# The second mixture's outputs sent from slots to tokens by scatter, with the last two batches planned anew

## The chip, the cores and the metric

The kernel runs on one core of a Trainium2 chip. The metric is the device time of one launch in microseconds; the median of three runs is given. All numbers below come from those runs and from one further execution, recorded by the hardware profiler.

The core has TensorE (PE; its weight loads are listed apart as PEld), VectorE (DVE), ScalarE (ACT), GpSimd (POOL) and SyncE (SP). SP issues nearly all plain transfers and GpSimd all indirect ones. Sixteen DMA engines carry both.

## The reference

The input x has 8 sequences of 512 tokens, 128 wide, that is 4096 tokens. With LN for a layer norm without weights:

```
xn = LN(x)
s  = mamba(xn)        # projection, causal conv, a scan of 16 states for each of 256 channels, projection, norm, MLP
g  = silu(ffn0(xn))   # first mixture: 24 experts, top 2, two expert layers, 4 groups of tokens
x1 = x + s * g
xn = LN(x1)
s1 = attention(xn)    # causal, 8 heads of 128, after an RMS norm
y  = ffn1(xn)         # second mixture: 128 experts, top 2, one layer
out = x1 + s1 * silu(y)
```

The second mixture is what the change is about. Each expert has 32 places ("slots") for tokens that have it as first choice and 32 for those that have it as second; second choices count behind all first choices. A token beyond its expert's capacity is dropped:

```
v1, v2 = loc1 < 32, loc2 < 32
idx1, idx2 = e1 * 32 + min(loc1, 31), e2 * 32 + min(loc2, 31)
buf[idx1] += x * v1 ; buf[idx2] += x * v2
yb = buf (per expert, 32 x 128) @ we[expert]
y  = g1 * v1 * yb[idx1] + g2 * v2 * yb[idx2]
```

g1 and g2 are the two softmax weights, divided by their sum. loc2 starts at the number of all first choices of the expert, so a second choice's place is known only when all 4096 tokens are routed.

## The kernel before, in words

A batch is one sequence: 512 tokens, as four tiles of 128 rows (NJ = 4). Everything is float32 unless said otherwise.

**First part.** The first mixture runs expert by expert (`expert1` L435, `between` L453, `expert2` L504). Rows come by gathers of GpSimd (L128); each expert adds its bias by a small bf16 matmul with one-hot columns (L516 in `expert2`) ahead of the four products of L518. ScalarE's copy of an expert's transposed input is L444. `routing` also fills the table `xs_dram` with zeros (L405). Beside it the model part of the scan goes forward in steps (`front` L549, `scan` L589, `gated` L645, `back` L661). There are 64 steps, eight per batch. A step loads two states of B and C from memory (`bb`, `cb`), computes `da` on ScalarE (L601) and on VectorE a product (L603), scans (L605) and a second product (L606), and adds up on TensorE (`py`, L627). `front` approximates a logarithm by four squares on ScalarE (L581), each with an operation of VectorE (L582). `squares` in the change is the list of these.

**Middle part.** For each batch `fetch` (L522) and `after` (L537) bring together the first mixture's output (`o`, rows gathered by GpSimd at L131) and the scan's output (`sb`, `xb`) into x1. `Attention.prepare` (L747) norms x1, computes the 128 router logits, picks two experts per token and ends in `route` (L788). `route` counts places by prefix sums and sends each token's normed row to its two slots: eight scatters of GpSimd per batch (L828) into `xs_dram[0]` (first choices) and `xs_dram[1]` (second choices), with a spare row for dropped tokens. A table `row1` (from `pos` and `e12`) keeps where each token's two results will stand.

`Attention.heads` (L894) yields once per head. Per head: scores `sc` (L854), a mask with running minimum on VectorE (L856), exponentials on ScalarE (L860), transposes `pp` (L874) copied out as `pT` (L876), products `po` (L881), a reciprocal (L886) and `s` (L892). `values_of` (L832; `pv` L839, `v` L840) and the `qm` products (L846) belong to it too. After a batch's last head `s1` is stored.

The first six batches' heads (48) are emitted in turn with the scan steps that are left, in proportion: step by step the scan is kept level with heads out of 48. Batch b + 1 is fetched, gated and prepared at heads 1, 3 and 4 of batch b. The order of instructions on each engine follows this order of emission roughly; a scheduler moves an instruction ahead of others where it takes that one to be ready sooner.

```
    left = NSTEP - taken
    total = EARLY * HEADS
    for i in range(total):
        next(attention_steps)
        while (taken - (NSTEP - left)) * total < (i + 1) * left:
            step()
```

**Last part.** Then batch 7 is prepared, `weights2` (L912) turns router maxima into two weights per token for all batches, and `places` (L925) computes `live`: which second-choice slots lie behind the first choices. The list `second` is emitted one entry per head of batches 6 and 7: `slots` (L951) loads 512 slots of both tables and transposes them, `experts` (L968) multiplies eight experts' 64 slots each (`pye` L973), masks by `live` into `yb` (L975) and stores to `yb_dram` (L976). After the 16 groups of experts `finish` (L978) follows for batches 0 to 5, one per head, and for 6 and 7 at the very end. It gathers two rows per token (L128), multiplies by the weights (L990, L991), applies silu (L992), multiplies with `s1` (L993), adds x1 (L994) and stores the output (L995).

SP's queue holds all plain loads and stores in the order of emission, each behind the wait of the one ahead of it: `we` weights of the experts, `xg` of `slots`, `yb_dram` stores, the loads of `finish`, the output.

Of the kernel before, what the change touches and what calls it, by code (L numbers as in the profile page):

```python
# [33 lines left out]
S1 = E1 * C1  # L34
HEADS, DHEAD = 8, 128
# [12 lines left out]
def tile_kernel(ctx: ExitStack, tc: tile.TileContext, t: dict, out: bass.AP):  # L48
# [42 lines left out]

    xs_dram = [dram.tile([S1 + P, D], F32, name=f"xs_dram{k}") for k in range(2)]
    yb_dram = dram.tile([2 * S1, D], F32, name="yb_dram")

# [75 lines left out]
    w121 = w3.tile([P, NTT, 2], F32, name="w121")  # L170
    row1 = w3.tile([P, NTT, 2], I32, name="row1")
    idx1 = w3.tile([P, NTT, 2], I32, name="idx1")
    kp1 = w3.tile([P, NTT, 2], F32, name="kp1")
# [21 lines left out]
    bias = inv_pool.tile([3 * 32, DH + D], BF16, name="bias")  # L195
    zero = inv_pool.tile([P, L], F32, name="zero")
    G.memset(zero, 0.0)
# [106 lines left out]
    eb = xp.tile([3 * 32, DH + D], F32, name="eb", bufs=1)  # L304
    G.memset(eb, 0.0)
    for k in range(3):
        Q.dma_start(eb[32 * k : 32 * k + E0, 0:DH], t["eb1"])
        Q.dma_start(eb[32 * k : 32 * k + E0, DH:], t["eb2"])
    part = xp.tile([3 * 32, DH + D], BF16, name="part", bufs=1)
# [33 lines left out]
    def routing():  # L343
# [59 lines left out]
        for k in range(2):  # L403
            tc.keep_in_program_order(
                Q.dma_start(  # L405
                    xs_dram[k][0:S1, :].rearrange("(p n r) d -> p n (r d)", p=P, r=L // D),
                    bc(zero.unsqueeze(1), (P, S1 // L, L)),
                )
            )
# [25 lines left out]
    def expert1(e, w):  # L435

        we = w(e)
        px = ps_e.tile([P, SLOTS], F32, name="px", tag="pe")
        for c, r in enumerate(SROWS):
            xg = me.tile([CP, D], F32, name="xg", bufs=8)  # L440
            gather(xg[:r], xn_dram, inv[:r, c, e : e + 1])
            T.transpose(px[:, c * CP : c * CP + r], xg[:r], ident[:r, :r])  # L442
        xT = me.tile([P, SLOTS], F32, name="xTe", tag="xTe")
        S.copy(xT, px)  # L444
        hs = me.tile([CP, SG, DH], F32, name="hs", tag="big", bufs=4)
        for c, r in enumerate(SROWS):
            ph = ps_e.tile([CP, DH], F32, name="ph", tag="pe")
            T.matmul(ph[:r], chosen(e, r), bias[:, 0:DH], start=True, stop=False)
            T.matmul(ph[:r], xT[:, c * CP : c * CP + r], we, start=False, stop=True)  # L449
            S.activation(hs[:r, c, :], ph[:r], AF.Copy, scale=wsl[:r, c, e : e + 1])  # L450
        store(hs_dram, e, hs)
# [52 lines left out]
    def expert2(e, w):  # L504
# [4 lines left out]
        for c, r in enumerate(SROWS):  # L509
# [6 lines left out]
            T.matmul(po[:r, c, :], chosen(e, r), bias[:, DH:], start=True, stop=False)  # L516
            for f in range(NJ):
                T.matmul(po[:r, c, :], hT[:, f, :r], we[:, f, :], start=False, stop=(f == NJ - 1))  # L518
# [28 lines left out]


    def front(b):  # L549
# [30 lines left out]
        for i in range(4):  # L580
            S.activation(sq, ex, AF.Square, bias=l1p[:, i : i + 1], scale=LOG1P_S)  # L581
            V.scalar_tensor_tensor(lp, sq, LOG1P[i][1], ex if i == 0 else lp, ALU.add, ALU.mult)  # L582
# [157 lines left out]
    class Attention:  # L740
# [6 lines left out]
        def prepare(self, b, xb):  # L747

            at, (ps_x, px) = self.at, self.ps_x
            xn2 = at.tile([P, NJ, D], F32, name="xn2", bufs=1)  # L750
            layernorm(st, xb, xn2, NJ, eps5, "ln1")
            pt = ps_x.tile([P, L], F32, name="pt2", tag=px)
            for j in range(NJ):
                T.transpose(pt[:, j * P : (j + 1) * P], xn2[:, j, :], ident)
# [15 lines left out]

            sq = at.tile([P, NJ, D], F32, name="sq2", bufs=1)
            ss = st.tile([P, NJ], F32, name="ss2")
            for j in range(NJ):
                S.activation(sq[:, j, :], xn2[:, j, :], AF.Square, accum_out=ss[:, j : j + 1])
# [4 lines left out]
            V.tensor_tensor(sq, xn2, bc(ss.unsqueeze(2), (P, NJ, D)), ALU.mult)  # L779
# [8 lines left out]
        def route(self, b, xn2):  # L788
# [28 lines left out]
            kp = kp1[:, bs, :]  # L817
# [5 lines left out]
            for k in range(2):  # L823
                V.tensor_scalar(pos[:, :, k], pos[:, :, k], float(C1 - 1), float(k * C1), ALU.min, ALU.add)
            V.scalar_tensor_tensor(row1[:, bs, :], e12, float(2 * C1), pos, ALU.mult, ALU.add)  # L825
# [87 lines left out]
    def weights2():  # L913
        V.reciprocal(se1, se1)
        V.tensor_tensor(w121, mx1[:, :, 0:2], bc(mx1[:, :, 0:1], (P, NTT, 2)), ALU.subtract)
        S.activation(w121, w121, AF.Exp)
        V.tensor_tensor(w121, w121, bc(se1.unsqueeze(2), (P, NTT, 2)), ALU.mult)
        den = r3.tile([P, NTT], F32, name="den1")
        V.tensor_tensor(den, w121[:, :, 0], w121[:, :, 1], ALU.add)
        V.tensor_scalar(den, den, EPS32, None, ALU.max)  # L920
        V.reciprocal(den, den)
        V.tensor_tensor(w121, w121, bc(den.unsqueeze(2), (P, NTT, 2)), ALU.mult)
        V.tensor_tensor(w121, w121, kp1, ALU.mult)

    def places():  # L925


        pair = r3.tile([P, 2], F32, name="pair")
# [19 lines left out]
        V.tensor_scalar(live, pk, c, float(C1), ALU.add, ALU.is_lt)  # L948


    def slots(t):  # L951
        for k in range(2):
            xg = mo.tile([P, 4, D], F32, name="xg1", bufs=4)
            Q.dma_start(xg, rows(xs_dram[k][t * L : (t + 1) * L, :]))
            px = ps_x.tile([P, 4, P], F32, name="pxs", tag="px")
            for j in range(4):
                T.transpose(px[:, j, :], xg[:, j, :], ident)
# [11 lines left out]
    def experts(e0, we):  # L969
# [6 lines left out]
        Q.dma_start(rows(yb_dram[2 * C1 * e0 : 2 * C1 * (e0 + 8), :]), yb)  # L976

    def finish(b):  # L978
# [4 lines left out]
        y = mo.tile([P, NJ, D], F32, name="y", tag="y")  # L983
        for j in range(NJ):
            i = b * NJ + j
            ya = mo.tile([P, D], F32, name="ya", tag="row", bufs=6)
            yc = mo.tile([P, D], F32, name="yc", tag="row", bufs=6)
            gather(ya, yb_dram, row1[:, i, 0:1])
            gather(yc, yb_dram, row1[:, i, 1:2])
            V.tensor_scalar(ya, ya, w121[:, i, 0:1], None, ALU.mult)  # L990
            V.scalar_tensor_tensor(y[:, j, :], yc, w121[:, i, 1:2], ya, ALU.mult, ALU.add)  # L991
# [70 lines left out]
    for n, of in mixture():  # L1062
        due += n / of
        while due > 0.5:
            step()
            due -= 1.0
    moe.close()
# [21 lines left out]
    def early():  # L1089
        for b in range(EARLY):  # L1090
            for hd, _ in enumerate(beside.heads(b, ready[b])):
                if hd == 1:
                    got = fetch(b + 1)
                if hd == 3:
                    xb = after(b + 1, *got)
                if hd == 4:
                    ready[b + 1] = beside.prepare(b + 1, xb)
                yield

    left = NSTEP - taken  # L1100
    total = EARLY * HEADS
    attention_steps = early()
    for i in range(total):
        next(attention_steps)
        while (taken - (NSTEP - left)) * total < (i + 1) * left:
            step()
    for _ in model_steps:
# [16 lines left out]
    live = r3.tile([P, E1 // 2], F32, name="live")  # L1124
    loaded = {e0: load_experts(e0) for e0 in range(0, 32, 8)}
    last = Attention(at, m_qk, w_vo, (ps_x, "px"), (ps_q, "pq"), (ps_s, "ps"), (ps_t, "pt"), (ps_o, "po"))
    for b in range(EARLY + 1, B):
        ready[b] = last.prepare(b, after(b, *fetch(b)))
    weights2()
# [17 lines left out]
    for b in range(EARLY):  # L1147
        second.append([lambda b=b: finish(b)])
# [5 lines left out]
    for b in range(EARLY, B):  # L1154
# [67 lines left out]
```

## Time and profile before

| | |
|---|---|
| median of 3 runs | 1572.94 us (1572.57 to 1575.37) |
| the profiled execution, its own time | 1575.27 us |
| its span from first to last instruction | 1573.6 us |
| mean granted TensorE clock | 0.899 |
| last operation of the scan (L606) ends | 1323.8 us |
| batch 7's last scatter index is ready | 1405.8 us |
| last store of `yb_dram` issued | 1481.2 us |
| first and last gather of `finish` | 1484.2 and 1565.2 us |
| DMA queues: q1, q10 (plain), q0 (indirect), MB | 99.39, 67.12, 51.01 |

The profile's span is cut into windows below. A window's row gives its bounds, its length, then for each engine its busy time and in brackets its number of instructions, then the granted clock, the busy share of the 16 DMA engines and GB/s. A row of the costliest groups names the line, the engine, the operation, the tiles that it writes and reads, its shape and count; behind the bar its busy time and the mean of one in ns; behind the second bar the idle time of its engine just ahead of it and what ended that.

### The profile page before, as it was taken

How to read it: one execution, taken by the hardware profiler on the slowest of the kernel's cores; microseconds unless marked ns; L12 is line 12 of the kernel's file. 1: busy time of each engine (PE TensorE's matmuls, PEld its weight loads, DVE VectorE, ACT ScalarE, POOL GpSimd, SP SyncE). 2: the span in 40 equal slices, each digit the busy share in tenths (PEclk: the TensorE clock that was granted, in tenths of full speed). 3: DMA queues.
4: the chain of work that ended last, by engine and by line, in shares of the span. 5: the costliest groups of instructions: out<-in, count | busy, mean ns of one | idle time of the engine just before them, and what ended most of it. 6: DMA issues, size and time to landing. Idle time of an engine off the chain costs nothing.

```text
span 1573.6 us, 20658 instructions
## 1 busy us (share of the span) xinstructions
PE 1227.2 (78%) x6825; PEld 864.5 (55%) x6825; DVE 1244.0 (79%) x2758; ACT 977.6 (62%) x1727; POOL 596.9 (38%) x502
## 2 busy tenths in 40 slices
PE   6786889522379889655889888989889899898974
PEld 4453445221357877533566665766657567566653
DVE  5629676778967757877999999999989999475565
ACT  5126667666667686554785857767578575563363
POOL 1234554456445434273712542025043301120176
PEclk9978989855699999776998999999989999999987
DMA  6265776877658756433322233114113230149344
GB/s 183 76 237 197 240 240 224 261 250 247 222 170 254 241 163 205 144 84 100 78 79 74 66 101 105 41 67 114 58 35 73 68 101 4 53 128 258 86 116 120
DMA packets 170669, 218.84 MB, mean 139 GB/s; under 512 B 16618, under 2 KB 118074, under 8 KB 170562
## 3 DMA queue, kind: packets, MB, share of 16 engines
q1 hardware_dynamic: 126018, 99.39, 20.5%
q10 hardware_dynamic: 18432, 67.12, 12.9%
q0 software_dynamic: 26112, 51.01, 12.3%
q8 instruction: 54, 0.88, 0.2%
q14 instruction: 53, 0.43, 0.1%
HBM read 161.56 MB, written 55.84 MB: 138 GB/s over the span
## 4 chain that ended last, share of the span: by engine, by line
DVE 36%; PE 31%; DMA 10%; ACT 7%; POOL 7%; issue 7%; SPq 1%; ACTq 0%; POOLq 0%; DVEq 0%
DVE u L605 11%; DVE u L606 5%; PE po L881 4%; PE sc L854 4%; DVE u L603 3%; DVE sc L856 3%; PE py L627 3%; POOL o L131 3%; PE ph L449 2%; PE pp L874 2%; PE po L518 2%; DMA bb<-xd_dram 2%; DVE s L892 2%; DMA yc<-yb_dram,row 2%; PE pc L559 2%
## 5 line engine op out<-in xcount | busy, mean ns | idle before, releaser
L605 DVE TENSOR_TENSOR_SCAN u<-da,u 128x512 f32<-128x512 f32 x256 | 312.5, 1241 | 54.8 <-ACT da L601 54.8
L627 PE MATMUL py<-ident,u 128*128 128x128 f32 x1024 | 164.6, 302 | 128.2 <-DVE u L606 128.2
L627 PEld LDWEIGHTS py<-ident,u 128*128 128x128 f32 x1024 | 132.3, 155 | 181.4 <-DVE u L606 162.2
L881 PE MATMUL po<-v,pT 128*128 128x129 f32 x1280 | 185.1, 287 | 20.1 <-DVE s L892 11.9
L601 ACT ACTIVATE da<-dt,a_neg 128x512 f32<-128x512 f32 x256 | 176.2, 719 | 36.0 <-DVE u L605 29.8
L881 PEld LDWEIGHTS po<-v,pT 128*128 128x128 f32 x1280 | 167.1, 199 | 49.5 <-issue 22.3
L854 PE MATMUL sc<-xaT,qm 128*128 128x128 f32 (+3 forms) x512 | 180.0, 461 | 12.4 <-ACT prob L860 9.9
L860 ACT ACTIVATE prob<-sc,mn 128x128 f32<-128x128 f32 (+3 forms) x256 | 130.1, 527 | 93.7 <-DVE mn L856 81.4
L603 DVE TENSOR_TENSOR u<-bb,lp 128x1024 f32<-128x1024 f32 x128 | 153.5, 1219 | 18.9 <-DMA bb<-xd_dram 18.9
L606 DVE TENSOR_TENSOR u<-u,cb 128x1024 f32<-128x1024 f32 x128 | 158.1, 1235 | 1.1
L856 DVE CUSTOM_DVE_ANT_0 sc<-sc,mask 128x128 f32<-128x128 f32 (+3 forms) x256 | 124.3, 496 | 23.1 <-PE sc L854 20.9
L131 POOL DMA_INDIRECT o<-os_dram,row x64 | 112.4, 1757 | 78.2 <-DMA bb<-xd_dram 30.9
L828 POOL DMA_INDIRECT xs_dram<-xn,idx x64 | 76.9, 1202 | 165.3 <-DVE row L825 74.0
L128 POOL DMA_INDIRECT xg<-xn_dram,inv x72 | 92.7, 1288 | 121.3 <-PE px L442 61.1
L874 PE MATMUL pp<-ident,prob 128*128 128x128 f32 x640 | 111.9, 284 | 26.9 <-DVE pT L876 22.6
L874 PEld LDWEIGHTS pp<-ident,prob 128*128 128x128 f32 x640 | 79.4, 145 | 85.5 <-issue 31.3
L128 POOL DMA_INDIRECT hg<-hid_dram,inv x72 | 89.7, 1246 | 95.4 <-PE pht L513 65.8
L854 PEld LDWEIGHTS sc<-xaT,qm 128*128 128x128 f32 x512 | 84.2, 198 | 56.3 <-ACT prob L860 26.3
L128 POOL DMA_INDIRECT hd<-hs_dram,row x64 | 81.9, 1280 | 64.3 <-DMA qkv_w<-in_qkv_w 23.7
L518 PEld LDWEIGHTS po<-we,hgT 128*128 128x128 f32 (+1 forms) x576 | 72.6, 191 | 19.3 <-issue 13.1
L518 PE MATMUL po<-we,hgT 128*128 128x128 f32 (+1 forms) x576 | 81.2, 289 | 1.9 <-ACT hgT L515 1.8
L876 ACT COPY pT<-pp 128x384 f32<-128x384 f32 (+1 forms) x100 | 51.4, 514 | 48.2 <-PE pp L874 47.7
(289 smaller groups left out, 2565.2 us busy)
## 6 DMA issues: line engine op xcount, KB each, us to landing
bb<-xd_dram ACTq DMA_DIRECT2D x64, 512.0 KB
cb<-xd_dram ACTq DMA_DIRECT2D x64, 512.0 KB
we<-in_W SPq DMA_DIRECT2D x48, 256.0 KB
hs_dram<-hs SPq DMA_DIRECT2D x24, 512.0 KB
hid_dram<-hd SPq DMA_DIRECT2D x32, 256.0 KB
we<-in_we SPq DMA_DIRECT2D x16, 512.0 KB
hs_dram<-hs SPq DMA_DIRECT2D x24, 192.0 KB
xb<-in_x SPq DMA_DIRECT2D x16, 256.0 KB
```

The source lines that it names most:

```text
L128: G.indirect_dma_start(dst, None, table[:, :], IOA(idx, 0))
L131: G.indirect_dma_start(dst, None, table[:, :], IOA(idx, 0), compute_op=ALU.add)
L518: T.matmul(po[:r, c, :], hT[:, f, :r], we[:, f, :], start=False, stop=(f == NJ - 1))
L601: S.activation(da[:, j, :], dt[:, hf, :], AF.Exp, scale=a_neg[:, hf, n0 + j : n0 + j + 1])
L603: V.tensor_tensor(u, bb, bc(dx[:, hf : hf + 1, :], (P, NC, L)), ALU.mult)
L605: V.tensor_tensor_scan(u[:, j, :], da[:, j, :], u[:, j, :], 0.0, ALU.mult, ALU.add)
L606: V.tensor_tensor(u, u, cb, ALU.mult)
L627: T.matmul(py[:, i, hf * P : (hf + 1) * P], us[hf][:, j, i * P : (i + 1) * P], ident, is_transpose=True, start=False, stop=(n0 + j == DS - ...
L854: T.matmul(sc[:, :w], qm[:, i * P : w], xaT[:, :w], start=True, stop=True)
L856: V.tensor_tensor_reduce(sc[:, :w], sc[:, :w], mask[:, L - w :], -1.0, FMAX, ALU.add, ALU.min, mn[:, i : i + 1])
L874: T.transpose(pp[:, c, :], prob[i][:, k * P : (k + 1) * P], ident)
L881: T.matmul(po[:, i - i0, :], pT[:, i * (i + 1) // 2 + k, :], v[:, k, hd % 4, :], start=(k == 0), stop=(k == i),)
```

## The change

The outputs of the second mixture now go from the slots to the tokens. `experts` scatters each slot's result, times the token's weight, to the token's own row of a table `y_dram` (4 scatters of 128 rows per group of eight experts, 64 in all, declared free of order among themselves). `finish` then loads two plain tiles (first and second choices) and adds them.

For that each row of `xs_dram` carries four more columns: weight and home row for either choice (`more` in `prepare`). `weights2` goes; its work is done per batch in `prepare`. `places` loads weights and homes of all slots with four transfers. The tables of slots are first filled with an `empty` row, whose home is -1; such slots go to rows of `y_dram` of their own behind the tokens' rows (`own`). `y_dram`'s token rows are zero-filled near the end of the first mixture, since dropped tokens get no row.

The plan of the batches is made anew. The scan steps are spread over 42 heads (LAST) instead of 48, and the scan is ended there. Batch 6 is fetched, gated and prepared at heads 37, 38 and 39, batch 7 at 42, 43 and 43; before, batch 7 came behind all 48. All eight `finish` are emitted behind the last head; in the built order the first ones' loads and adds still stand among the last six heads' instructions.

Two smaller edits go with it. The bias of the first mixture's second layer comes by four-byte transposes of a broadcast column instead of the bf16 matmul with three-part one-hot rows. And the first expert's copy (L444) is put behind the four squares of `front(0)` on ScalarE.

The diff, cut to its core:

```diff
+DX = D + 4
+NY = NTOK + S1
...
-    xs_dram = [dram.tile([S1 + P, D], F32, name=f"xs_dram{k}") for k in range(2)]
-    yb_dram = dram.tile([2 * S1, D], F32, name="yb_dram")
+    xs_dram = [dram.tile([S1 + P, DX], F32, name=f"xs_dram{k}") for k in range(2)]
+    y_dram = dram.tile([2 * NY, D], F32, name="y_dram")
...
+    home = w3.tile([P, NTT, 2], F32, name="home")
+    home_i = w3.tile([P, NTT, 2], I32, name="home_i")
+    G.iota(home_i, pattern=[[P, NTT], [NY, 2]], base=0, channel_multiplier=1)
+    V.tensor_copy(home, home_i)
...
+    empty = inv_pool.tile([P, 2, DX], F32, name="empty")
+    G.memset(empty, 0.0)
+    for k in range(2):
+        G.memset(empty[:, k, D + 2 * k + 1 : D + 2 * k + 2], -1.0)
...
-                    xs_dram[k][0:S1, :].rearrange("(p n r) d -> p n (r d)", p=P, r=L // D),
-                    bc(zero.unsqueeze(1), (P, S1 // L, L)),
+                    xs_dram[k][0:S1, :].rearrange("(p n) d -> p n d", p=P),
+                    bc(empty[:, k : k + 1, :], (P, S1 // P, DX)),
...
-        S.copy(xT, px)
+        copied = S.copy(xT, px)
+        if e == 0:
+            follows(copied, squares[3])
...
-            T.matmul(po[:r, c, :], chosen(e, r), bias[:, DH:], start=True, stop=False)
+
+            T.matmul(
+                po[:r, c, :], bc(bias2[:, e : e + 1], (P, r)), ident, is_transpose=True, start=True, stop=False,
+                skip_group_check=True,
...
-            S.activation(sq, ex, AF.Square, bias=l1p[:, i : i + 1], scale=LOG1P_S)
+            squares.append(S.activation(sq, ex, AF.Square, bias=l1p[:, i : i + 1], scale=LOG1P_S))
...
+            V.reciprocal(se1[:, bs], se1[:, bs])
+            w12 = st.tile([P, NJ, 2], F32, name="w121")
+            V.tensor_tensor(w12, mx1[:, bs, 0:2], bc(mx1[:, bs, 0:1], (P, NJ, 2)), ALU.subtract)
+            S.activation(w12, w12, AF.Exp)
+            V.tensor_tensor(w12, w12, bc(se1[:, bs].unsqueeze(2), (P, NJ, 2)), ALU.mult)
+            den = st.tile([P, NJ], F32, name="den1")
+            V.tensor_tensor(den, w12[:, :, 0], w12[:, :, 1], ALU.add)
+            V.tensor_scalar(den, den, EPS32, None, ALU.max)
+            V.reciprocal(den, den)
+            more = xn2[:, :, D:].rearrange("p j (k a) -> p j k a", a=2)
+            V.tensor_tensor(more[:, :, :, 0], w12, bc(den.unsqueeze(2), (P, NJ, 2)), ALU.mult)
+            V.tensor_copy(more[:, :, :, 1], home[:, bs, :])
...
-            for k in range(2):
-                V.tensor_scalar(pos[:, :, k], pos[:, :, k], float(C1 - 1), float(k * C1), ALU.min, ALU.add)
-            V.scalar_tensor_tensor(row1[:, bs, :], e12, float(2 * C1), pos, ALU.mult, ALU.add)
...
+        more = r3.tile([P, E1 // 2, 2], F32, name="more")
+        for a in range(2):
+            for k in range(2):
+                h = 2 * C1 * a + C1 * k
+                Q.dma_start(
+                    more[h : h + C1], xs_dram[k][0:S1, D + 2 * k : D + 2 * k + 2].rearrange(
+                        "(q a c) d -> a c q d", a=2, c=C1)[a]
...
+                )
...
+        V.tensor_tensor(live, live, more[:, :, 0], ALU.mult)
+
+        own_i = r3.tile([P, E1 // 2], I32, name="own_i")
+        for a in range(2):
+            for k in range(2):
+                h = 2 * C1 * a + C1 * k
+                G.iota(own_i[h : h + C1], pattern=[[2 * C1, E1 // 2]], base=NTOK + NY * k + C1 * a, channel_multiplier=1)
+        own = r3.tile([P, E1 // 2], F32, name="own")
+        V.tensor_copy(own, own_i)
+        V.scalar_tensor_tensor(own, more[:, :, 1], 0.0, own, ALU.is_lt, ALU.mult)
+        V.scalar_tensor_tensor(to, more[:, :, 1], 0.0, own, ALU.max, ALU.add)
...
-        Q.dma_start(rows(yb_dram[2 * C1 * e0 : 2 * C1 * (e0 + 8), :]), yb)
+        for j in range(4):
+            q = e0 // 2 + j
+            sent = G.indirect_dma_start(y_dram[:, :], IOA(to[:, q : q + 1], 0), yb[:, j, :], None)
+            tc.declare_no_dep(sent.ins, group="sent", reason="no two slots have the same row")
+            tc.add_to_no_dep_group("sent", sent.ins)
...
-        y = mo.tile([P, NJ, D], F32, name="y", tag="y")
-        for j in range(NJ):
-            i = b * NJ + j
-            ya = mo.tile([P, D], F32, name="ya", tag="row", bufs=6)
-            yc = mo.tile([P, D], F32, name="yc", tag="row", bufs=6)
-            gather(ya, yb_dram, row1[:, i, 0:1])
-            gather(yc, yb_dram, row1[:, i, 1:2])
-            V.tensor_scalar(ya, ya, w121[:, i, 0:1], None, ALU.mult)
-            V.scalar_tensor_tensor(y[:, j, :], yc, w121[:, i, 1:2], ya, ALU.mult, ALU.add)
+        y = mo.tile([P, NJ, D], F32, name="y")
+        Q.dma_start(y, rows(y_dram[b * L : (b + 1) * L, :]))
+        y2 = mo.tile([P, NJ, D], F32, name="y2")
+        Q.dma_start(y2, rows(y_dram[NY + b * L : NY + (b + 1) * L, :]))
+        V.tensor_tensor(y, y, y2, ALU.add)
...
+    for k in range(2):
+        tc.keep_in_program_order(
+            Q.dma_start(
+                y_dram[k * NY : k * NY + NTOK, :].rearrange("(p n) d -> p n d", p=P),
+                bc(empty[:, 0:1, 0:D], (P, NTOK // P, D)),
+            )
+        )
...
-            for hd, _ in enumerate(beside.heads(b, ready[b])):
-                if hd == 1:
-                    got = fetch(b + 1)
-                if hd == 3:
-                    xb = after(b + 1, *got)
-                if hd == 4:
-                    ready[b + 1] = beside.prepare(b + 1, xb)
-                yield
+            yield from beside.heads(b, ready[b])
+    LAST = EARLY * HEADS - 6
+    got, gates = {}, {}
+    def begin(b):
+        got[b] = fetch(b)
+    def gate_of(b):
+        gates[b] = after(b, *got[b])
+    def make_ready(b):
+        ready[b] = beside.prepare(b, gates[b])
+    plan = {}
+    for b in range(1, B):
+        at_head = {B - 2: LAST - 5, B - 1: LAST}.get(b, HEADS * (b - 1) + 1)
+        for i, what in zip((0, 2, 3) if b < B - 2 else (0, 1, 2) if b < B - 1 else (0, 1, 1), (begin, gate_of, make_ready)):
+            plan.setdefault(at_head + i, []).append((what, b))
     left = NSTEP - taken
-    total = EARLY * HEADS
     attention_steps = early()
-    for i in range(total):
+    for i in range(EARLY * HEADS):
         next(attention_steps)
-        while (taken - (NSTEP - left)) * total < (i + 1) * left:
+        while (taken - (NSTEP - left)) * LAST < (i + 1) * left and taken < NSTEP:
             step()
+        if i == LAST - 1:
+            for _ in model_steps:
+                pass
+        for what, b in plan.get(i, ()):
+            what(b)
...
-    for b in range(EARLY + 1, B):
-        ready[b] = last.prepare(b, after(b, *fetch(b)))
-    weights2()
...
-    for b in range(EARLY):
-        second.append([lambda b=b: finish(b)])
...
-    for b in range(EARLY, B):
+    for b in range(B):
```

## The prediction

> **What bounds the kernel now.** I read the page first, then stage windows, then what each late engine waits for. The page's first part and its chain:
>
> ```profile
> PE 1227.2 (78%) x6825; PEld 864.5 (55%) x6825; DVE 1244.0 (79%) x2758; ACT 977.6 (62%) x1727; POOL 596.9 (38%) x502
> DVE 36%; PE 31%; DMA 10%; ACT 7%; POOL 7%; issue 7%; SPq 1%; ACTq 0%; POOLq 0%; DVEq 0%
> ```
>
> No engine is the bound everywhere. The windows (after the stretch and its length: PE, PEld, DVE, ACT, POOL busy, clock, DMA share) show which one is where:
>
> ```profile
> 900.00:1000.00 100.00, 90.50 (x462) 59.77 (x463) 96.28 (x250) 71.86 (x124) 33.66 (x26) 0.97 0.32 88
> 1100.00:1200.00 100.00, 88.20 (x468) 60.03 (x468) 93.99 (x235) 67.70 (x109) 33.21 (x24) 0.95 0.21 59
> ...
> 1323.00:1480.00 157.00, 144.00 (x953) 101.82 (x952) 94.38 (x319) 75.89 (x152) 22.21 (x23) 0.99 0.46 127
> 1480.00:1574.00 94.00, 58.10 (x281) 41.51 (x280) 54.00 (x182) 42.87 (x66) 62.25 (x64) 0.83 0.38 108
> ```
>
> Up to 1323 us, where the last scan operation (L606) ends, VectorE holds the time (94 to 98 in 100) with TensorE at 88 to 91. From there to 1480, attention and the second experts run on TensorE (144 of 157 us). In the last 94 us nothing is full: the gathers of `finish` pace it. The groups of 1480 to 1574 say so:
>
> ```profile
> L128 POOL DMA_INDIRECT yc<-yb_dram,row x32 | 31.6, 987 | 10.2 <-issue 9.6 <-DMA yc<-yb_dram,row 0.6
> L128 POOL DMA_INDIRECT ya<-yb_dram,row x32 | 30.7, 958 | 75.4 <-DMA yb_dram<-yb 66.0 <-issue 4.3 <-DVE y L994 1.2
> ...
> L991 DVE SCALAR_TENSOR_TENSOR y<-yc,w,ya 128x128 f32<-128x128 f32 x32 | 11.1, 349 | 11.4 <-DMA yc<-yb_dram,row 8.9 <-DVE y L991 1.3 <-DVE mn L856 0.5
> L990 DVE TENSOR_SCALAR ya<-ya,w 128x128 f32<-128x128 f32 x32 | 9.3, 292 | 17.8 <-DMA ya<-yb_dram,row 17.6
> ```
>
> GpSimd's first gather waited 66.0 us for the last `yb_dram` store, then 64 of them follow at 0.95 to 0.99 us plus 0.30 of issue, 1565 us being the last. VectorE, which also serves the heads, stands 17.6 + 8.9 us behind them.
>
> **Behind the scan: what goes.** TensorE is idle 251 - 202.1 = 49 us from 1323 to the end (144.0 + 58.1 busy): 13 before 1480, 36 after. The 64 gathers, the 32 L990 and 32 L991 (9.3 + 11.1 us of VectorE) and the 16 `yb_dram` stores on SP go; two plain loads per batch and eight adds (about 0.69 us each by the L994 row) come. So the 36 us go: **-36**. What is late next is the end of attention itself, because every `finish` is now emitted behind the last head: the last `s` (L892, 0.34), the store of `s1` and its reload (2.3 us as for the last `yb` store, 2.8 as for an `xg` load), two operations of 0.69 and the last 3.3 us of the span (store issued at 1570.29, span end 1573.6) make 10 to 11: **+11**. The `y` loads of the other batches stand on SP behind batch 6's `s1` store and beside the heads; all eight batches' `s1`, `x1`, `y`, `y2` and `out` are 8 x 1.25 MB = 10.5 MB, 35 us at the 300 GB/s seen while experts load, within the last six heads' 43 us. Bufs of two make the third batch's load wait for the first one's store; I take nothing, bounds 0 to +8.
>
> **The 64 scatters of `y`** use GpSimd as the 64 gathers did: 1.27 us cadence as the eight L828 scatters of batch 7 (1406.3 to 1417.1, with one wait), 81 us. They now lie beside the experts, four per group of eight experts. The order of instructions spreads the 16 groups over heads 48 to 56.5, about 61 us of TensorE work, 70 at its real pace. So GpSimd is nearly as slow as its source; three `yb` buffers hold 3 groups. A late scatter only holds `yb`, then the `pye` bank, then a head. Zero, bounds 0 to +8.
>
> **The plan.** Scan steps are dealt over 42 heads instead of 48. In the instruction order 44.5 heads stood ahead of the last scan operation and now 38.5 do. VectorE loses there six to seven heads. Between 760 and 1322 us its head rows are L856 0.50 + 0.14, L876 0.59, L840 0.68, L892 0.34, L886 0.16; by the counts of the order (6.5 heads' masks, 24 `s`, 13 reciprocals, 14 `pT`, 8 `v`, less 7 small operations per `prepare` and the three removed) that is 32 us net: **-32**. TensorE does not lose that work. Costed by rows (`sc` 0.46, `pp` 0.28, `po` 0.29 each, `pv` 0.6, `pqm` 0.73 and so on, with overlap taken off), what lies behind the scan rises from about 177 to 230 us: **+53**. That is the heart of it: in the scan stage a head costs 4.5 to 5 us of the bounding engine, behind it 7.2 to 8.8 of the other.
>
> `prepare(6)` now runs with hardly any attention beside it on VectorE; before, `prepare(7)` and the end of `back(7)` stood so. `prepare(7)` is freed of the `we` loads ahead of `sb` on SP (6.4 us from issue to landing at 1375.42). The 13 us of idle before 1480 therefore stay: 0, bounds -8 to +8.
>
> **The new wait: `more`.** Four SP loads read weight and home row of every slot, 2048 runs of 8 bytes each, 8192 in all, 512 on each of 16 engines, after the last `xs_dram` scatter. The `live` of places (VectorE) waits for them; behind it in VectorE's order stand every mask and `pT` of the heads, so TensorE starves once one head is used up; on SP the first `xg` loads stand behind too. No row of before has 8-byte runs to 32 partitions. From below: isolated loads of 8 to 32 bytes at the start take 9 ns of an engine, 512 x 9 = 4.6 us. Nearest in place: in the window 1417 to 1424, where just these rows are loaded as 512-byte packets,
>
> ```profile
> q1 hardware_dynamic: 2381, 1.19, 58.3%
> ```
>
> 0.583 x 7 x 16 / 2381 = 27 ns a packet, 14 us. The page's whole row, 126018 packets in 20.5%, gives 41 ns, 21 us, and 60 ns would be 31. The Trainium skill speaks against this load (DMA: Bandwidth & Descriptors, Rules for kernel authors): a strided last dimension becomes one descriptor per element, so keep it contiguous; under Bandwidth, Measured, it has a floor of about 10.5 ns a packet, from which I estimate 5.4 us, all hidden. I take between row and rule, nearer the row: 20 to 27 ns, 10 to 14 us, plus 2.3 to land the last scatter, 13 for the eight scatters, some 26 from the last index on. VectorE has about 15 us of head work between the last index and `live`. **+11**, bounds 0 and +25.
>
> **The first 700 us.** `follows` puts the first expert's copy behind the four squares. VectorE waited there:
>
> ```profile
> DVE lp L582 <- ACT work L581: 19.6, 3, 17.1
> ```
>
> 17.1 us, with two `xTe` copies ahead of the third square. But `da` still stands behind both copies: -3 to -5, at most -8. The zero fill of `xs_dram` has 528-byte rows in place of 2048: 8192 descriptors, +2 to +3 ahead of the copies. The two new fills of `y_dram` (2 x 2.1 MB, 10 us at 400 GB/s, the rate of that first fill) share the 16 engines and SP's queue ahead of `sb` and `o` loads near 650 us: +2, bounds 0 to +8. Bias two: L516 (227 ns as modelled, some 60 apart) becomes a 4-byte transpose (`pht` row 283, some 110 apart), 72 x 0.05 = 3.6 us of TensorE at most; half of it beside waits, +2 at most. Sum **-1**, bounds -6 and +6. The seven small operations of each `prepare` are in the -32.
>
> **Sum.** -1 - 32 + 53 - 36 + 11 + 11 = +6. The span goes from 1573.6 to about 1580; the profiled run, 1.7 over its span at 1575.3, to 1581; the median, 1572.9, to 1579.
>
> **Rivals.** *Faster (0.35).* TensorE, not only VectorE, is relieved in the scan stage. VectorE's 3 to 6 idle us per 100 there are partly waits for TensorE (`sc` 4.8, `rsum` 6.1, `pT`, `v` in the rows of 760 to 1322). If the thinner mix lets VectorE run at 99 in 100 over 520 us, the scan ends 16 us sooner than I say: -10, about 1563. It decides from 6 us on. Against it: the order puts no fewer masks per step ahead of each scan. *The load of `more` hides* (in that 0.35 and in the next): with the floor of 9 to 10 ns nothing waits, -11: 1568. *No change (0.13)*: half of either, 1573. *Slower by the small loads (0.17)*: 50 to 60 ns a run makes 26 to 31 us, all the cover is used up and TensorE stands 25: 1593. *Scatters or `finish` loads become the bound (0.07)*: +8 each: 1590 to 1595. *The change doesn't do what it says:* the tail still idles 36 us because the plain loads wait for the last scatter: 1600, small, since the last group lies seven heads before the end.
>
> **The numbers.** Likeliest, 1579 by the sum, with 0.28 of its own; with the small loads and the two other bounds slower has 0.52, no change 0.13, faster 0.35. About 0.2% (1569.8 to 1576.1) is what a measurement of this kernel can tell from no change. Below, -10 with the hidden load reaches 1560; above, +25 for `more` in place of 11 with a few us of the other bounds, 1598. The slower cases' own range is 1576 to 1598.
>
> **What would show it.** In the profile after: the last L606 near 1290; TensorE busy some 255 us behind it; no indirect row in the last 60 us; the end 10 to 11 us behind the last `po`; `live` waiting on `more` some 11 us with TensorE idle beside it; 512 packets per engine of 20 to 27 ns; the first py some 5 us earlier. I am wrong if the scan ends before 1280, or if TensorE's idle time behind it is under 25 us.

## The result, and the profile after

The changed kernel takes 1596.64 us (median of 4 runs, 1594.62 to 1597.57); the kernel before took 1574.15 in the same comparison. The ratio is 1.0132, 95% interval 1.0098 to 1.0166: slower by 1.3%. The profiled execution took 1596.85 us, its span is 1595.1 (before 1575.27 and 1573.6). The forecast was 1579, slower; the span was to grow by 6 us and grew by 21.5. The direction is right, the amount more than three times the likeliest one.

The page's first part and chain of the changed kernel:

```profile
PE 1245.8 (78%) x6826; PEld 874.8 (55%) x6826; DVE 1226.5 (77%) x2726; ACT 981.4 (62%) x1745; POOL 588.2 (37%) x509
...
DVE 18%; PE 16%; DMA 4%; issue 2%; ACT 2%; POOL 2%; SPq 0%; POOLq 0%; DVEq 0%; ACTq 0%
```

The busy shares of the engines have hardly moved (before, PE 78%, DVE 79%), and this chain names only 44% of the span, so it can't say where the time went. The windows can (columns as before):

```profile
1100.00:1200.00 100.00, 87.32 (x477) 62.25 (x475) 95.16 (x232) 72.95 (x123) 33.88 (x23) 0.95 0.24 65
1295.20:1440.00 144.80, 124.29 (x640) 82.46 (x641) 83.45 (x312) 69.89 (x148) 27.55 (x33) 0.91 0.30 71
1440.00:1520.00 80.00, 79.77 (x564) 55.89 (x563) 42.00 (x123) 34.88 (x67) 49.93 (x54) 1.00 0.43 126
1520.00:1584.00 64.00, 50.70 (x290) 37.27 (x289) 42.29 (x126) 44.78 (x64) 6.71 (x8) 0.95 0.51 148
1584.00:1595.10 11.10, 0.07 (x1) 0.00 (x0) 2.16 (x5) 0.00 (x0) 0.00 (x0) 0.64 0.24 71
1295.20:1595.10 299.90, 254.83 (x1490) 175.62 (x1490) 169.91 (x566) 149.54 (x279) 84.19 (x93) 0.93 0.38 102
```

VectorE still bounds the scan stage (95.16 in 100), which now ends at 1295.2. Behind it stand 299.9 us in place of 249.8. While the experts run beside the heads, TensorE is full (79.77 of 80). The gathers are gone, and 36 us of idle TensorE with them, but 13.3 us of idle stand at 1520 to 1584 and 11.0 at the end. The same row for the kernel before, cut at the end of its scan:

```profile
1323.80:1573.60 249.80, 201.54 (x1229) 143.01 (x1228) 147.58 (x501) 118.18 (x216) 84.46 (x87) 0.93 0.43 121
```

So a span can be written as: end of the scan, plus TensorE's busy time behind it, plus its idle time behind it. This holds for any run, so it says where time lies and not why. Before: 1323.8 + 201.5 + 48.3. After: 1295.2 + 254.8 + 45.1. The change is -28.6 + 53.3 - 3.2 = +21.5.

The end of the scan has a scatter of its own. Two traces whose source is the same up to there have the first `po` (the first product of attention) at 755.9 and 761.0 us (the kernel before and the run below with the plan alone), and seven with the source of the changed kernel up to there have it between 753.6 and 760.6. From the first `po` to the end of the scan it is steadier: 567.9 us before, 540.8 after, 27.1 less.

What VectorE waited for from 1295 on, in us, times, longest (the two largest rows, waits for TensorE, come first):

```profile
DVE sc L885 <- PE sc L883: 37.6, 54, 5.3
DVE rsum L915 <- PE po L910: 30.0, 24, 3.0
...
DVE y L1028 <- DMA y<-y_dram: 8.8, 3, 7.7
...
DVE y L1030 <- DMA s1f<-s_dram: 5.3, 1, 5.3
DVE live L975 <- DMA more<-xs_dram: 4.2, 1, 4.2
```

`y L1028` is the first operation of `finish`. Its longest wait, 7.7 us, is one instruction in VectorE's order (timeline, first row), and TensorE's next transpose stands behind it (second row):

```profile
1535.39 0.69 DVE L1028 TENSOR_TENSOR y<-y,y 128x512 f32<-128x512 f32 x1 [7.70 <-DMA y<-y_dram]
```

```profile
1538.45 0.90 PE L903 MATMUL pp<-ident,prob 128*128 128x128 f32 x3 [6.17 <-DVE pT L905]
```

The `y` loads wait for the last scatter: it was issued at 1527.9, SP's first `y` load at 1531.6.

### The profile page after: what moved, and what is told of

Its sections match the earlier page's. It is cut to its first block, busy times and chain, and to the rows that moved or that the text cites. A ratio compares the mean times of both kernels' runs of the same rounds, so it can differ in the third digit from the quotient of the medians.

```text
span 1595.1 us, 20645 instructions
## 1 busy us (share of the span) xinstructions
PE 1245.8 (78%) x6826; PEld 874.8 (55%) x6826; DVE 1226.5 (77%) x2726; ACT 981.4 (62%) x1745; POOL 588.2 (37%) x509
## 5 line engine op out<-in xcount | busy, mean ns | idle before, releaser
L624 DVE TENSOR_TENSOR_SCAN u<-da,u 128x512 f32<-128x512 f32 x256 | 309.0, 1229 | 58.0 <-ACT da L620 57.7
L646 PE MATMUL py<-ident,u 128*128 128x128 f32 x1024 | 169.4, 304 | 133.4 <-DVE u L625 133.1
L622 DVE TENSOR_TENSOR u<-bb,lp 128x1024 f32<-128x1024 f32 x128 | 158.6, 1259 | 22.8 <-DMA bb<-xd_dram 22.8
L134 POOL DMA_INDIRECT o<-os_dram,row x64 | 116.1, 1814 | 77.7 <-DMA cb<-xd_dram 32.1
L131 POOL DMA_INDIRECT hg<-hid_dram,inv x72 | 85.1, 1182 | 95.2 <-PE pht L526 67.2
L883 PEld LDWEIGHTS sc<-xaT,qm 128*128 128x128 f32 x512 | 81.6, 195 | 52.6 <-ACT prob L889 24.5
L877 ACT COPY qm<-pqm 128x512 f32<-128x512 f32 x64 | 37.1, 583 | 73.3 <-PE pqm L875 71.3
L462 PE MATMUL ph<-we,xTe 128*128 128x512 f32 x144 | 73.3, 636 | 7.9 <-DMA we<-in_W 5.1
L535 PE MATMUL po<-we,hgT 128*128 128x128 f32 (+1 forms) x576 | 77.3, 280 | 1.6 <-ACT hgT L528 1.5
```

The costliest lines, as they stand in the source:

```text
L131: G.indirect_dma_start(dst, None, table[:, :], IOA(idx, 0))
L134: G.indirect_dma_start(dst, None, table[:, :], IOA(idx, 0), compute_op=ALU.add)
L622: V.tensor_tensor(u, bb, bc(dx[:, hf : hf + 1, :], (P, NC, L)), ALU.mult)
L624: V.tensor_tensor_scan(u[:, j, :], da[:, j, :], u[:, j, :], 0.0, ALU.mult, ALU.add)
L646: T.matmul(py[:, i, hf * P : (hf + 1) * P], us[hf][:, j, i * P : (i + 1) * P], ident, is_transpose=True, start=False, stop=(n0 + j == DS - ...
L883: T.matmul(sc[:, :w], qm[:, i * P : w], xaT[:, :w], start=True, stop=True)
```

## The experiments

Ratios are to the kernel before, timed in the same set of runs. The last four runs below (two of the fills, the bias, all together) are a set of their own. In it the kernel before took 1602.9 us, 1.6% more than in the other two sets (1577.1 and 1576.6), though the chip has the same number as in the first of these; why is not known. The changed kernel itself was not timed in that set, so these four ratios are compared with one another, and with 1.0132 only with care.

**The plan alone.** In the kernel before, the loop over the early batches and the preparing of batch 7 are replaced by those of the change.

```diff
-    total = EARLY * HEADS
+    LAST = EARLY * HEADS - 6
...
+        at_head = {B - 2: LAST - 5, B - 1: LAST}.get(b, HEADS * (b - 1) + 1)
...
-    for b in range(EARLY + 1, B):
-        ready[b] = last.prepare(b, after(b, *fetch(b)))
```

> The kernel before with the new plan of the batches alone: scan steps over 42 heads, batches 6 and 7 prepared at heads 37 to 43; gathers, stores and weights as before. Theory (the plan costs): the scan ends near 1298, TensorE is busy some 250 us behind it, the gathers still leave some 45 us idle; time 1590 to 1598. Rival (the plan is neutral or gains, since experts and gathers begin earlier): 1565 to 1575.

Measured: 1612.42 us, ratio 1.0209 (1.0163 to 1.0255), 14 us above the theory's time. The profiled execution is the longest of its four (1619.36; the shortest took 1605.72). Its scan ends at 1304.4; behind it:

```profile
1304.40:1617.70 313.30, 260.26 (x1461) 178.35 (x1459) 176.65 (x609) 148.52 (x272) 84.86 (x89) 0.90 0.35 97
```

1304.4 + 260.3 + 53.0. The scan ends 19 us earlier (24.5 earlier counted from the first `po`), TensorE has 59 us more behind it, and idle time grows by 5: the exchange is the one the theory names, but both terms behind the scan are larger than it said (250 and 45). The gathers now begin at 1518.7, not 1484.2, because the last `yb_dram` store, for which the first gather waits, is issued at 1515.7, not 1481.2; they still run 81 us.

**The scatters without the plan.** First with LAST at 48 in the new loop, then with the old loop put back word for word.

```diff
-    LAST = EARLY * HEADS - 6
+    LAST = EARLY * HEADS
...
-    for b in range(1, B):
+    for b in range(1, EARLY + 1):
```

> The changed kernel with the plan of the batches undone: scan steps dealt over 48 heads, batch 7 prepared behind them; scatters, plain loads and all small edits stay. Theory (the plan is what costs: six heads leave the stage where VectorE is the bound and come behind it, +53 of TensorE for -32 of VectorE): the scan ends near 1311, as its last operation now stands behind 42 heads in VectorE's order instead of 38.5; TensorE busy some 225 us behind it, idle some 40; time 1570 to 1580. Rival (the scatters and the plain loads cost the 22 us themselves, through the wait of the first y add and the wait for more): time 1590 to 1597, and the first y add still waits 7 us or more on VectorE.

Measured: 1610.69 us, ratio 1.0213 (1.0191 to 1.0235). Theory and rival both missed: undoing the plan in this way made the changed kernel slower. The new loop emits scan steps and the preparing of a batch in another order than the old one, and the scan ended at 1331.7, not at the 1311 expected, so this is no clean undoing. The next is:

> The changed kernel with the old loop over the early batches put back word for word (the run with 48 heads had its scan steps and batch 6 in another order than the kernel before); scatters, plain loads and small edits stay. Theory (with the old plan all 16 groups of experts stand within four heads of VectorE's order, so that the 64 scatters at 1.26 us, 81 us from the first yb on, become the bound, and TensorE stands behind yb): last scatter 80 us or so behind the first, VectorE waits 15 us or more for scatters at yb, time 1590 to 1605. Rival (only the other order of that run was slow; the scatters gain): 1563 to 1575.

Measured: 1590.76 us, ratio 1.0076 (1.0051 to 1.0100), at the low edge of what the theory said (the profiled execution, 1593.52, is the longest of its eight). Its span is 1327.1 + 212.0 + 52.7. The second row is the stretch from the first scatter to the last:

```profile
1327.10:1446.00 118.90, 107.68 (x596) 75.08 (x594) 73.43 (x291) 67.32 (x134) 22.88 (x27) 0.96 0.33 77
1446.00:1528.00 82.00, 65.20 (x485) 49.77 (x480) 32.18 (x89) 22.84 (x42) 61.94 (x64) 0.88 0.48 139
1528.00:1591.80 63.80, 39.06 (x223) 28.63 (x221) 40.10 (x113) 37.95 (x52) 0.00 (x0) 0.89 0.53 154
```

GpSimd's 64 scatters fill 80 of these 82 us, 0.97 us each and 0.3 us apart, and TensorE idles 16.8. The waits name the buffer:

```profile
DVE yb L1012 <- DMA y_dram<-yb,to: 22.9, 8, 5.2
...
DVE y L1028 <- DMA y<-y_dram: 9.7, 2, 8.7
...
PE pxs L994 <- DVE yb L1012: 16.8, 6, 4.8
```

**More buffers, later adds.** On the old loop with scatters: eight `yb` buffers; then also the adds of `finish` ordered behind 59 heads.

```diff
-        yb = mo.tile([P, 4, D], F32, name="yb", bufs=3)
+        yb = mo.tile([P, 4, D], F32, name="yb", bufs=8)
```

> As the one with the old loop, with eight yb buffers in place of three. Theory (the scatters hold TensorE through the yb buffers): VectorE's wait for scatters at yb falls to under 5 us and TensorE runs on, but the last scatter stays where GpSimd's 81 us put it, so that part comes back as a longer wait of the first y add, 10 us or more; 5 to 12 us faster than with three. Rival (GpSimd's floor alone sets the end): no gain.

Measured: 1586.15 us, ratio 1.0053 (1.0021 to 1.0085), not to be told from 1.0076. The wait at `yb` is gone and has come back in one place, from where it reaches TensorE:

```profile
DVE y L1028 <- DMA y<-y_dram: 33.5, 3, 32.5
...
PE pp L903 <- DVE pT L905: 35.6, 4, 30.9
```

33.5 us against 22.9 + 9.7 = 32.6 with three buffers: the wait was moved, not removed. The last scatter is issued 80 us behind the first in both runs (1448.7 to 1528.9 here), and that sets when `y` can be read.

> As the one with eight yb buffers, and the adds of finish ordered behind 59 heads. Theory (then neither scatters nor y loads hold the heads): VectorE's wait for y under 4 us, TensorE's idle time behind the scan near 30 us, time 1560 to 1575, at or below the kernel before. Rival (the adds pile up behind the last head): tail of 20 us or more, time 1580 to 1590.

Measured: 1585.79 us, ratio 1.0036 (1.0004 to 1.0068). The wait is still 27.4 us where the theory said under 4, and its time was missed by 10 us: ordering the adds behind 59 heads is not cover enough. The rival's time fits, its tail of 20 us does not (the last `po` ends 11.1 us before the end).

**Later adds in the changed kernel.** Here the adds stand behind 59 heads too, ahead of them 57.5 before.

```diff
-        V.tensor_tensor(y, y, y2, ALU.add)
+        follows(V.tensor_tensor(y, y, y2, ALU.add), heads_done[58])
```

> The changed kernel with the first add of every finish ordered behind the last head but five on VectorE (59 heads instead of 57.5 stand ahead of the first add). Theory (the first add is placed before its loads can land, and its wait of 7.7 us holds the masks and copies of the heads, so that TensorE stands 6.2 us): the wait on y falls under 2 us, TensorE's wait for pT falls by 6 or more, time 1584 to 1590. Rival (the adds only move: what they no longer hold in the middle comes behind the last head): wait gone but tail longer, time 1594 to 1598.

Measured: 1596.33 us, ratio 1.0120 (1.0097 to 1.0143), no difference that can be told from 1.0132. The wait for `y` fell from 8.8 to 1.8 us, and from 1500 on TensorE's wait for `pT` from 11.0 to 1.6; but its wait for `s`, which stands behind the adds in VectorE's order, grew from 1.6 to 5.7. Idle time from 1520 to the last `po` fell from 13.3 to 9.8 us, and the stretch behind the scan's end from 299.9 to 297.0. So taking the wait away is worth some 3 us at most. The rival is nearer.

**The small loads twice.** They go into two tiles, and one more operation of VectorE reads both.

```diff
-        for a in range(2):
+        for a, tile_ in ((0, more0), (1, more0), (0, more), (1, more)):
...
+        V.tensor_tensor(more[:, :, 0], more0[:, :, 0], more[:, :, 0], ALU.max)
```

> The changed kernel with the four loads of weights and homes issued twice, into two tiles, both read by the masking of the slots (one small maximum more). Theory (the loads cost what the trace shows: 6.5 us for 8192 runs of 8 bytes, all in front of the first slot loads, with VectorE's cover used up): VectorE's wait grows from 4.2 to 10 or 11 us and the time by 5 to 7, to 1601 to 1604. Rival (the experts lie far enough ahead of the end, so that later slot loads cost nothing and only VectorE's order matters, with work left to hide them): +0 to +2.

Measured: 1604.81 us, ratio 1.0167 (1.0137 to 1.0197); the ratio is 0.35% or 5.5 us above the changed kernel's, though the intervals overlap. VectorE's wait grew from 4.2 to 7.8 us, where the theory said 10 or 11, and `live` came 24.8 us behind the last scatter index instead of 18.6: the second set takes 6 us to load. What that costs is not shown. The profiled span is 7.4 us longer than the changed kernel's, but 4.9 of it stands ahead of the scan's end (1300.1), where the edit does nothing, and 2.5 behind it.

**The moved copy alone.** In the kernel before, only this (with the list `squares` kept in `front`):

```diff
-        S.copy(xT, px)
+        copied = S.copy(xT, px)
+        if e == 0:
+            follows(copied, squares[3])
...
```

> The kernel before with one edit alone: the first expert's copy behind the four squares on ScalarE. Theory (the 17.1 us wait of VectorE for the third square goes, but the first da still stands behind both copies): first da 1 to 4 us earlier, time 1 to 4 us shorter than before. Rival (all of the first 130 us is covered by what the mixture's experts need anyway): no difference.

Measured: 1564.07 us, ratio 0.9908 (0.9883 to 0.9934): faster than the kernel before by 12.6 us, where 1 to 4 were expected. The first scan comes at 112.7 instead of 122.5 us, the first `po` at 745.1 instead of 755.9, the scan ends at 1315.8 instead of 1323.8. ScalarE's timeline before (the first fence) and with the edit (the second):

```profile
106.68 0.45 ACT L444 COPY xTe<-px 128x352 f32<-128x352 f32 x1 [11.08 <-PE px L442]
112.46 0.45 ACT L444 COPY xTe<-px 128x352 f32<-128x352 f32 x1 [5.32 <-PE px L442]
112.80 1.15 ACT L581 ACTIVATE work<-work,l1p 128x1024 f32<-128x1024 f32 x1
...
118.95 1.33 ACT L601 ACTIVATE da<-dt,a_neg 128x512 f32<-128x512 f32 x2 [2.55 <-DVE dt L583]
```

```profile
97.43 1.15 ACT L585 ACTIVATE work<-work,l1p 128x1024 f32<-128x1024 f32 x1 [1.35 <-DVE lp L586]
105.42 0.45 ACT L444 COPY xTe<-px 128x352 f32<-128x352 f32 x1 [6.84 <-PE px L442]
111.58 0.45 ACT L444 COPY xTe<-px 128x352 f32<-128x352 f32 x1 [5.72 <-PE px L442]
111.93 2.56 ACT L605 ACTIVATE da<-dt,a_neg 128x512 f32<-128x512 f32 x4
```

The squares are done ahead of both copies, and `da` follows the second copy at once: 7 us at ScalarE, 10 at the first scan; of this lead 8.6 us is left in the profiled span.

**The fills.** The changed kernel's fill of `y_dram` is taken into the scan stage in 16 pieces; then that of `xs_dram` also, into the second half of the first mixture (the calls are shown).

```diff
+        if 4 <= i < 20:
+            fill_y(i - 4)
...
+            if 2 <= e < 18:
+                fill_xs(e - 2)
```

> The changed kernel with the zero fill of y_dram taken from the end of the first mixture into the scan stage, as 16 pieces of 262 KB, one per head from head 4 on. Theory (in the changed kernel the lead over the kernel with the moved copy alone goes from 2 us at the 128th scan to 9 us behind at the first attention product; the 4.2 MB on SP's queue and the 16 engines ahead of sb and o are the cause): first attention product 5 to 8 us earlier than in the changed kernel, time 4 to 8 us shorter, near 1590. Rival (what is lost there has another cause, the order of the prepared batch): no change.

Measured: ratio 1.0185 (1.0147 to 1.0224), no gain that shows. From the last `os_dram` store to the first `po` it is 106.4 us, in the changed kernel 106.1: the fill of `y_dram` costs nothing there. The rival holds, as far as these marks go.

> As the one before, and the zero fill of xs_dram (528-byte rows) taken from the start of the first mixture into its second half, as 16 pieces of 270 KB, one per expert. Theory (the fill of 8192 rows stands ahead of the first experts' rows, so that the two copies ahead of the first da come 6 us later and eat what the moved copy had won): first scan near 112 as with the moved copy alone (118 in the changed kernel), all later marks 4 to 9 us earlier than with the y fill alone moved, time near 1583. Rival (the pieces take from the second half what the start gains): no further change.

Measured: ratio 1.0114 (1.0073 to 1.0154). The first scan comes at 116.1 us (119.4 with the `y` fill alone moved), the 33rd at 219.2 (226.0), the 65th at 389.5 (398.1), the first `po` at 757.4 (761.4). So without the early fill of `xs_dram` these marks come 3 to 9 us earlier, and 4 us of it are left at the first `po`. The median is 9.7 us below that of the run before (1624.3 and 1634.0), and five of its six executions lie below all six of the other; the profiled one is the sixth, so the two profiled spans (1629.2 and 1626.6) do not show the gain. The intervals just overlap: a gain at the end of the kernel is likely and not settled.

**The bias.** The changed kernel with the bf16 matmul of the kernel before for the second layer.

> The changed kernel with the bf16 matmul for the second layer's bias put back. Theory of the prediction (72 transposes cost up to 0.05 us more each): 0 to 2 us faster than the changed kernel. Rival (the trace shows the second layer of experts over in 190.2 us after, 194.8 before, so the transposes are no cost or a gain): 0 to 4 us slower than the changed kernel.

Measured: ratio 1.0179 (1.0133 to 1.0224), which decides neither way, as the changed kernel was not timed in this set. Its first `da` is at 113.5 us (117.6 in the changed kernel). All 14 traces agree on where this comes from: GpSimd's first gather for the first expert starts at 95.0 to 97.0 us in the four with the bf16 bias and at 100.2 to 102.0 in the ten with the transposed one. They also differ between the last `os_dram` store and the first `po`: 102.7 to 103.8 us against 105.5 to 109.2. So the new bias goes with 4 to 5 us at the start and some 3 before attention; how it makes them was not tried.

**All together.** Old loop, scatters, five `yb` buffers, both fills moved, three buffers in `finish`, adds behind 61 heads.

> The best version that the runs point to: old plan, scatters with five yb buffers, both fills moved as above, three buffers for the tiles of finish, adds ordered behind 61 heads. Theory (each of the terms adds up): scan ends near 1316, first scatter near 1435, last near 1515, the adds no longer hold the heads; time 1555 to 1570, below the kernel before. Rival (the adds of eight batches pile up behind the last heads): 1575 to 1585.

Measured: ratio 1.0178 (1.0133 to 1.0222). Theory and rival both missed: the scan ended at 1339.0 where 1316 was expected, and the scatters took from 1457.6 to 1564.0, 106 us in place of 80. The moved copy alone is the best of the versions that were run.

## Why the prediction was right, and where it was off

**What luck had in it.** The 1596.64 us lie inside the stated range, but close to its upper end, and that end stood on `more` costing 25 us in place of 11. `more` cost less than 11; other terms filled the range. The miss of the span is 15.5 us: 4.4 at the end of the scan, 0.3 in TensorE's busy time, 10.8 in its idle time.

**The exchange of the plan.** Right in mechanism and nearly in size. The scan ends 28.6 us earlier (forecast 33, near 1290; it is 1295.2), and TensorE has 53.3 us more behind it (forecast 53). The term of 32 us for VectorE is 27.1 counted from the first `po`. The plan alone shows the same exchange, 24.5 for 59 by the same count. The six heads cost the scan stage less than they cost behind it.

**The idle time is the step that was off.** Forecast -36 + 11 + 11 = -14; measured -3.2. Its terms: the tail is 11.0 us, as said. The stretch to 1440 has 20.5 us idle, where 13 + 11 were said. And 13.3 us at 1520 to 1584 were put at nothing (bounds 0 to +8): "Bufs of two make the third batch's load wait for the first one's store; I take nothing". What waited longest was the first add, not the third (7.7 us, of which TensorE's row has 6.2): its loads depend on the last of 64 scatters, and VectorE's order has the add ahead of the heads' copies. A rival named this dependence and called it small, "since the last group lies seven heads before the end". But the add's turn came no later: VectorE was free for it at 1527.7, before the last scatter was issued. How much time the wait cost stays open: with the adds later, 9.8 of the 13.3 us of idle time stayed, part of it behind the wait for `s`.

**The scatters** were put at zero, since GpSimd was taken to be nearly as slow as its source. It was a little faster: the 64 took 99.3 us (1428.6 to 1527.9), and GpSimd waited 21.4 of them for `yb`. In the changed kernel no wait at `yb` is among the larger ones. But that holds only with the new plan: with the old one the scatters are the bound of their stretch (22.9 us at `yb`, 16.8 us of idle TensorE). So the parts do not add. By medians, in us: the plan alone +35, the rest of the change with the old loop +14, both +22. The account that the rows suggest: the plan spreads the experts over more heads, which hides the scatters (80 us with the old plan, 99 with the new), and the scatters take away the gathers, which the plan had pushed back.

**The wait for `more`** was put at 11 us and is 4.2 on VectorE, 3.3 on TensorE. In the window 1401 to 1410 of the changed kernel, where these loads run:

```profile
q1 hardware_dynamic: 8443, 0.16, 57.3%
```

That is 0.573 x 9 x 16 / 8443 = 9.8 ns a packet, with other packets among them. The trace's own records of the 8192 packets of 8 bytes give 8.9 ns each, the first starting at 1404.2 and the last at 1409.3 us. The prediction had the right neighbour in hand, the 9 ns of short loads at the start of the trace with their 4.6 us, and set it aside for the row of 512-byte packets. That row was the wrong one, since the time grows with the bytes: packets of 128, 320 and 512 bytes in the first 40 us of the kernel before have a median of 13, 20 and 27 ns. The figure of about 10.5 ns a packet that the Trainium skill gives for its smallest transfer (DMA: Bandwidth & Descriptors, Bandwidth, Measured) is near, though it is for loads issued from GpSimd and these come from SP. The skill's rule that a strided last dimension becomes one descriptor per element (same page, Rules for kernel authors) did not bear on this load: its last dimension is two floats side by side, and there is one packet for each pair, not one for each float. Still the load is not free: `live` comes 18.6 us behind the last scatter index instead of 0.4, and most of that lay under other work.

**The first 700 us** came out at -1.5 (first `po` 754.4 against 755.9), forecast -1. That is luck: the terms were wrong and cancelled, and this mark scatters by 5 to 7 us. The moved copy alone is worth 10.8 there, not 3 to 5: it was priced by ScalarE's wait for the copies alone, which end as late as before, while the third and fourth squares, the dependent VectorE operations and `dt` behind them also went under that wait. Against it stand the early fill (2 to 3) and the bias (2). In the changed kernel ScalarE's first copy comes 8 us later than with the moved copy alone:

```profile
113.44 0.45 ACT L455 COPY xTe<-px 128x352 f32<-128x352 f32 x1 [13.56 <-DMA xs_dram<-empty]
```

```profile
112.99 0.37 PE L453 MATMUL px<-ident,xg 96*128 96x96 f32 x1
```

The first row names the fill as what released the copy, but the second shows the last transpose of the copy's own input ending at 113.36, just ahead of it, so the fill need not be what the copy waited for. The bias run has the same early fill and its first copy at 109.0: some 3.5 us of the 8 are left for the fill, as the run with both fills moved says too (3.3 at the first scan), and 4.5 go with the bias, which was priced by TensorE's time alone. The fill of `y_dram` (2) is nothing.

**The rivals.** The faster one, a relieved TensorE that lets VectorE run at 99 in 100, did not come: between 755 and 1290 VectorE is busy 508.2 of 535 us, 515.8 before. The slower one by small loads did not come either. What came is nearest to the small cases at 1590 to 1600, `finish` loads that become a bound or wait for the last scatter, though with 13 us of idle time and not 36.

## What to carry to other kernels

Price a moved piece of work twice, on the engine that bounds the stage it leaves and on the one that bounds the stage it enters; here 28.6 us were bought with 53.3. A scatter in place of a gather moved the same GpSimd time (64 pieces, some 80 us) to the producer's side, and the first reader then waited for the last scatter: look where that reader stands in its engine's order. Parts that share such a resource do not add, so measure each part alone: one small reordering inside this change was worth 0.9% by itself, and the whole change hid it. And before a mark of one trace is explained, look how far that mark moves between traces of the same source.

## What the runs showed that was not expected

Reads of 8 bytes, 8192 of them on 16 engines, took 8.9 ns each in the mean, a third of the 27 ns of 512-byte packets. VectorE's waits for the last scatters and the loads behind them changed place more than size: 32.6, 33.5 and 27.4 us under three arrangements of buffers and order. In the last set of runs the same 64 scatters of the new plan took 126 us (1431.0 to 1557.6 in the run with the bf16 bias) where they took 99 in the changed kernel. From 1430 to 1550 TensorE idled 16.6 of 120 us there at a granted clock of 0.91, where the changed kernel had 0.23 idle in 80 at 1.00. Why that set differs was not tried.
